# Two swapped neighbours in a hand-written order of steps: a block product against the first product of the next gate, and a vector add against a gate step

## The chip, the cores and the metric

The kernel runs on one core of one Trainium2 chip. The metric is the device time of that core in microseconds (us), from launch to end, as the median of several runs. Five engines work on the core side by side, each in its own order: TensorE (PE in the profile, with its weight loads shown apart as PEld), VectorE (DVE), ScalarE (ACT), GpSimd (POOL), and SyncE (SP), which here only issues transfers.

## What is computed

128 graphs of 128 nodes with 256 features go through four graph layers: attention with four heads, a gated graph network, a relational layer, attention with one head. Each layer is followed by a residual sum and a layer norm. The change lies in the second layer, a GRU that runs three rounds with one set of gate weights:

```python
A = (adj != 0).astype(x.dtype)
h = x
for i in range(3):
    m = jnp.einsum('bnd,de->bne', h, weight[i])
    aggr = jnp.einsum('bst,bsd->btd', A, m)
    gi = aggr @ w_ih.T + b_ih            # i_r, i_z, i_n
    gh = h @ w_hh.T + b_hh               # h_r, h_z, h_n
    r = sigmoid(i_r + h_r)               # reset gate
    z = sigmoid(i_z + h_z)               # update gate
    n = tanh(i_n + r * h_n)              # new state
    h = (1.0 - z) * n + z * h
```

## The kernel before

**Groups and steps.** The graphs are cut into 33 groups: one of 2 graphs, 31 of 4, one of 2. Each stage of the work on one group is a Python generator, and every `yield` ends one step of it. `loads` (L160) brings a group in, `head` (L432) is the first layer, `chunk_0` and `chunk_1` (L680, L683, both through `chunk`, L630) are the two halves of the 256 hidden features of the GRU, `reset_and_new` (L624) and `new_and_update` (L627) make its gates, and `tail` (L686) does the last two layers and the store.

**The order is written out by hand.** Strings of letters say which generator takes its next step. `STEPS` (L61) is one period, 356 letters; the loop at L850 plays it 31 times, each time with the groups moved on by one. In `PERIOD` (L60) a letter names a stage and how far its group lies from that of the period. For the change four letters matter, all of the period's own group: `b` is `chunk_0`, `d` is `chunk_1`, `f` is `reset_and_new`, `g` is `new_and_update`. Since a step emits its instructions when it is called, and L857 to L867 tie each engine's instructions together in the order written, the letters fix the order on every engine. There is no scheduler. `START` and `END` hold what comes before the first and after the last period.

**The gates.** `gates` (L578) multiplies the 2 x 2 blocks of a gate's weights with the 2 x 2 blocks of the state in seven block products, the weight blocks in `factors` and the state's blocks and their sums in `layer[source]`. `f` makes the reset gate r (14 steps in each round) and then the input's part of the new state, "ni" (10 steps); `g` makes the hidden part of the new state, "nh" (10 steps), and then the update gate z (14 steps). A gate takes two PSUM banks of two halves each: `first` holds c11 and c12 (tag `sums`), `second` holds c21 and c22 (tag `gate`). There are two banks of each tag, taken in turn. So z gets the very banks that nh had before it, and z's first product may write only once ScalarE has read nh out of them. In r and z each product comes twice, once for the hidden state (`h`) and once for what the neighbours send (`a`); ni has only `a`, nh only `h`. The steps of a gate, as far as they matter here:

```python
for i, source in enumerate(TERMS[name]):
    product(c21, 1, source, start=i == 0)      # first block product
    yield
    product(c22, 5, source)                    # second block product
    yield
nc.scalar.copy(c11, c21)                       # L600
nc.scalar.copy(p5, c22)                        # L602
yield
... 
nc.vector.tensor_add(c12, c21, p5)             # L610
yield
for source in TERMS[name]:
    product(c12, 3, source)
yield
```

All products are `nc.tensor.matmul` at L590. [...] In the names of the profile `T_a` and `T_h` are sums of state blocks, `agT` is what the neighbours sent, `h0T` and `h2T` are the state after no and after two rounds, and `p_ni`, `p_z` are the `p5` of those gates.

**The two halves of the state.** In `chunk` each round goes: tanh of r on ScalarE (L642), nh out of PSUM on ScalarE (L648), `n = (r + 1) * n` on VectorE (L650), add ni (L652, VectorE), tanh (L654, ScalarE), `d = h - n` (L657, GpSimd), tanh of z (L642), and the new state (L662 and L663, VectorE). L676 copies a transposed state out of PSUM on ScalarE.

Of the kernel before, what the change touches and what calls it, by code (L numbers as in the profile page):

```python
# [58 lines left out]
"""  # L59
PERIOD = {"a": ("v", -1), "b": ("u", 0), "c": ("h", 1), "d": ("v", 0), "e": ("t", -2), "f": ("p", 0), "g": ("q", 0), "h": ("l", -1), "i": ("t", -1), "j": ("t", -3), "k": ("l", 2), "l": ("h", 2), "m": ("l", 0), "n": ("l", 1)}  # L60
STEPS = """  # L61
abcbddbedfggffghgdbiffgecfffdfdfjccccgfffggfbcjgbbgedcdidfgffgffeggfgifcbffegigggjfeibbkggdbgiiecccc
eggbdbibdfcdiiicfgggibeiicbdilbbiifciiickiidgddfiddfgddegfffffieggemginifdfcfibcgifcbdldlcclifffdgge
efggbfcgfgegggecfgfbgfcbfgcdbgbdbgiccclddbfbigdbbcccciddgbbffgiccddddcfdgfigfffffcccccdiffgeggffiggd
dibcfegfiigggffbfbggdfgfggbbfigbgffbldbggdiliilelgddlcil
"""
LAST = {"a": ("v", -2), "b": ("u", -1), "c": ("v", -1), "d": ("p", -1), "e": ("q", -1), "f": ("t", -3), "g": ("t", -2), "h": ("t", -4), "i": ("t", -1), "j": ("l", -2), "k": ("l", -1)}
END = """
# [864 lines left out]
```

## Time and profile before

| What | Value |
|---|---|
| median of 3 runs | 2881.12 us (2878.44 to 2882.46) |
| the profiled execution, its own time | 2883.62 us |
| its span, first to last instruction | 2881.8 us |
| its mean granted TensorE clock | 0.994 |
| PE busy | 2769.5 us, 96% of the span |
| PEld busy | 2287.3 us, 79% |
| DVE busy | 2291.2 us, 80% |
| ACT busy | 1735.7 us, 60% |
| POOL busy | 941.0 us, 33% |

How to read it: a busy share is an average over the whole span. Time is lost where TensorE, in its fixed order, stands before an instruction whose input or whose bank is not ready. The profile lists such idle time under the engine that waited, with what ended it. A weight load runs ahead of its matmul, so a wait often shows as longer idle time on PEld than on PE.

One period of the order lasts 86.5 us: the same matmul, z's first product in the first round, starts at 1073.43 us and at 1159.95 us.

### The profile page before, as it was taken

What the parts mean: (1) busy time and instruction counts of PE and PEld (TensorE: products, weight loads), DVE (VectorE), ACT (ScalarE), POOL (GpSimd) and SP (SyncE); (2) the same over time, 40 slices, a digit from 0 to 9 for tenths busy, and PEclk for the clock granted to TensorE, in tenths of its full rate; (3) what the DMA queues carried; (4) which work ended last, traced back from release to release, by engine and by line L of the source; (5) the groups of instructions that cost most, each with busy time, mean ns of one, the idle gap of its engine ahead of it and who ended that gap; (6) DMA issues with size and microseconds to landing.
All of it is one profiled execution on the core that took longest, in us unless ns stands there. A gap on an engine that the chain in (4) does not pass through costs nothing.

```text
span 2881.8 us, 44849 instructions
## 1 busy us (share of the span) xinstructions
PE 2769.5 (96%) x14486; PEld 2287.3 (79%) x14486; DVE 2291.2 (80%) x5334; ACT 1735.7 (60%) x4440; POOL 941.0 (33%) x925
## 2 busy tenths in 40 slices
PE   6899999999999999999999999999999999999986
PEld 4778888888888888888888888888888888888774
DVE  6677887878887878887878887878888877887765
ACT  3556666556666656666656666656666656666544
POOL 0224333323333323333323333323333423333331
PEclk9999999999999999999999999999999999999998
DMA  3344555444545444545344445344445444445321
GB/s 93 76 82 84 97 103 107 84 92 88 99 99 110 81 92 90 102 96 112 83 89 93 98 96 114 86 83 97 95 96 114 89 80 98 94 96 108 70 56 45
DMA packets 1179216, 264.01 MB, mean 92 GB/s; under 512 B 932064, under 2 KB 1178720, under 8 KB 1178976
## 3 DMA queue, kind: packets, MB, share of 16 engines
q1 hardware_dynamic: 1174448, 257.26, 44.5%
q10 hardware_dynamic: 4528, 3.81, 0.5%
q8 instruction: 118, 1.93, 0.3%
q14 instruction: 122, 1.00, 0.1%
HBM read 153.36 MB, written 107.61 MB: 91 GB/s over the span
## 4 chain that ended last, share of the span: by engine, by line
PE 74%; DVE 19%; issue 2%; ACT 2%; POOL 1%; DMA 1%; SPq 0%; DVEq 0%; POOLq 0%; ACTq 0%
PE gate L590 34%; PE ps L115 20%; PE sums L590 16%; DVE d L662 2%; PE ps L118 2%; DVE h3T L663 2%; DVE gate L618 2%; DVE h2T L663 2%; DVE n L652 1%; DVE aT L512 1%; DVE em L475 1%; DVE h0T L334 1%; DVE em L796 1%; POOL T_h L553 1%; DVE sums L610 1%
## 5 line engine op out<-in xcount | busy, mean ns | idle before, releaser
L590 PE MATMUL gate<-T_a,factors 128*128 128x256 f32 (+1 forms) x2376 | 683.1, 376 | 18.1 <-DVE T_a L553 17.3
L590 PE MATMUL gate<-T_h,factors_h 128*128 128x256 f32 (+1 forms) x2376 | 682.0, 377 | 12.3 <-DVE gate L618 8.9
L590 PEld LDWEIGHTS gate<-T_a,factors 128*128 128x128 f32 x2376 | 438.6, 190 | 91.5 <-DVE T_a L553 29.9
L590 PEld LDWEIGHTS gate<-T_h,factors_h 128*128 128x128 f32 x2376 | 428.6, 190 | 96.2 <-DVE gate L618 37.3
L590 PE MATMUL sums<-agT,factors 128*128 128x256 f32 (+1 forms) x1188 | 356.0, 381 | 5.5 <-ACT sums L600 1.4
L654 ACT ACTIVATE n<-n,bih 128x512 f32<-128x512 f32 (+1 forms) x198 | 139.6, 705 | 258.0 <-DVE n L652 258.0
L600 ACT COPY sums<-gate 128x256 f32<-128x256 f32 (+1 forms) x396 | 139.8, 353 | 228.6 <-PE gate L590 223.3
L590 PEld LDWEIGHTS sums<-agT,factors 128*128 128x128 f32 x1188 | 214.9, 190 | 63.5 <-ACT sums L600 16.8
L361 ACT ACTIVATE x<-x,mr_x,rs_x 128x256 f32<-128x256 f32 x384 | 199.2, 589 | 90.9 <-DVE mr_x L356 90.9
L398 ACT ACTIVATE em<-em,nm 128x128 f32<-128x128 f32 x640 | 248.2, 392 | 8.2 <-DVE nm L395 5.3
L657 POOL TENSOR_TENSOR d<-h1T,n 128x512 f32<-128x512 f32 (+1 forms) x66 | 82.1, 1245 | 500.2 <-ACT n L654 500.2
L715 POOL TENSOR_TENSOR x<-x,x 128x512 f32<-128x512 f32 x63 | 78.9, 1273 | 457.9 <-DVE x L712 255.1
L115 PE MATMUL ps<-wh,aT 128*128 128x64 f32 (+1 forms) x1280 | 191.0, 296 | 1.5 <-DVE aT L512 1.0
L657 POOL TENSOR_TENSOR d<-h2T,n 128x512 f32<-128x512 f32 (+1 forms) x66 | 92.7, 1405 | 286.3 <-ACT n L654 286.3
L590 PE MATMUL gate<-agT,factors 128*128 128x256 f32 (+1 forms) x594 | 180.4, 385 | 3.3 <-ACT r L642 2.5
L115 PEld LDWEIGHTS ps<-wh,aT 128*128 128x128 f32 x1280 | 170.7, 192 | 13.5 <-DVE aT L512 1.2
L573 ACT COPY agT<-ps 128x512 f32<-128x512 f32 (+1 forms) x198 | 114.0, 576 | 97.9 <-PE ps L115 97.7
L650 DVE SCALAR_TENSOR_TENSOR n<-r,n 128x512 f32<-128x512 f32 (+1 forms) x198 | 129.8, 669 | 52.4 <-ACT n L648 52.2
L354 POOL TENSOR_TENSOR rs_x<-rs_x,neghalf 128x4 f32<-128x4 f32 (+1 forms) x99 | 98.5, 995 | 217.4 <-DVE rs_x L353 217.3
L745 POOL TENSOR_TENSOR x<-x,b 128x256 f32<-128x256 f32 x128 | 138.3, 1110 | 68.4 <-PE ps L115 68.4
L610 DVE TENSOR_TENSOR sums<-gate,p_r 128x256 f32<-128x256 f32 (+1 forms) x99 | 42.0, 425 | 141.6 <-PE gate L590 141.5
L115 PE MATMUL ps<-w,x0s 128*128 128x264 f32 x512 | 139.2, 396 | 14.9 <-DMA factors_h<-in_L_gnn_w_hh_dram 14.9
(169 smaller groups left out, 6258.1 us busy)
## 6 DMA issues: line engine op xcount, KB each, us to landing
d_em<-em SPq DMA_DIRECT2D x63, 512.0 KB, 3.4
aT<-d_em SPq DMA_DIRECT2D x252, 128.0 KB, 3.9
x0s<-in_x_dram SPq DMA_DIRECT2D x248, 64.0 KB, 2.5
adj<-in_adj_dram SPq DMA_DIRECT2D x62, 256.0 KB, 3.9
x<-in_x_dram SPq DMA_DIRECT2D x31, 512.0 KB, 4.0
d_h0T<-x SPq DMA_DIRECT2D x62, 256.0 KB, 2.8
h0T<-d_h0T SPq DMA_DIRECT2D x124, 128.0 KB, 3.2
d_h<-h3T SPq DMA_DIRECT2D x62, 256.0 KB, 2.3
```

Of the source, the lines that this page charges most:

```text
L115: nc.tensor.matmul(ps, lhsT, rhs, start=start, stop=stop)
L354: nc.gpsimd.tensor_tensor(rs, rs, neghalf[:, :n], ALU.pow)
L361: nc.scalar.activation(y[:, g, :], y[:, g, :], AF.Identity, bias=mr[:, g : g + 1], scale=rs[:, g : g + 1])
L398: nc.scalar.activation(em[:, r, :], em[:, r, :], AF.Exp, bias=nm[:, i : i + 1], accum_out=den[:, i : i + 1])
L573: nc.scalar.copy(t, ps)
L590: nc.tensor.matmul(into, w[:, SEL[name], k - 1], layer[source][k], start=start, stop=True, skip_group_check=True)
L600: nc.scalar.copy(c11, c21)
L650: nc.vector.scalar_tensor_tensor(n, tr, 1.0, n, ALU.add, ALU.mult)
L654: nc.scalar.activation(n, n, AF.Tanh, bias=bih[:, 2 * C + c : 2 * C + c + 1])
L657: nc.gpsimd.tensor_sub(d, hT, n)
L663: nc.vector.scalar_tensor_tensor(hT, d, 0.5, n, ALU.mult, ALU.add)
L745: nc.gpsimd.tensor_add(x2[:, g, :], x2[:, g, :], b2)
```

## The change

Three lines of letters differ, in three places, each an exchange of two neighbouring letters (positions count from 0):

```
position  58: "g f" becomes "f g"
position 246: "d b" becomes "b d"
position 320: "d f" becomes "f d"
```

```diff
 STEPS = """
-abcbddbedfggffghgdbiffgecfffdfdfjccccgfffggfbcjgbbgedcdidfgffgffeggfgifcbffegigggjfeibbkggdbgiiecccc
+abcbddbedfggffghgdbiffgecfffdfdfjccccgfffggfbcjgbbgedcdidffgfgffeggfgifcbffegigggjfeibbkggdbgiiecccc
 eggbdbibdfcdiiicfgggibeiicbdilbbiifciiickiidgddfiddfgddegfffffieggemginifdfcfibcgifcbdldlcclifffdgge
-efggbfcgfgegggecfgfbgfcbfgcdbgbdbgiccclddbfbigdbbcccciddgbbffgiccddddcfdgfigfffffcccccdiffgeggffiggd
-dibcfegfiigggffbfbggdfgfggbbfigbgffbldbggdiliilelgddlcil
+efggbfcgfgegggecfgfbgfcbfgcdbgbdbgiccclddbfbigbdbcccciddgbbffgiccddddcfdgfigfffffcccccdiffgeggffiggd
+dibcfegfiigggffbfbggfdgfggbbfigbgffbldbggdiliilelgddlcil
 """
```

Counting the letters gives the steps. At 58, `f` takes its 16th step, ni's second block product in the first round (`product(c22, 5, "a")`), and `g` its 11th, z's first block product (`product(c21, 1, "h", start=True)`): on TensorE ni's product now stands ahead of z's. At 246, `d` takes its 30th step, L662 and L663 of the second round on VectorE, and `b` its 29th, the copy of L676 on ScalarE: two engines, so the order on each stays what it was. At 320, `d` takes its 41st step, L650 of the third round for the second half, and `f` its 68th, L610 for ni: on VectorE the add now stands ahead of L650. No step that is exchanged issues a transfer. The orders on ScalarE, GpSimd and SyncE are unchanged, and so are `START` and `END`.

## The prediction

> **What bounds the kernel now.** I read the page's busy rows first, then the chain that ended last, then the list of waits, and last the timeline at the two places where the order of an engine changes.
>
> ```profile
> PE 2769.5 (96%) x14486; PEld 2287.3 (79%) x14486; DVE 2291.2 (80%) x5334; ACT 1735.7 (60%) x4440; POOL 941.0 (33%) x925
> ...
> PE 74%; DVE 19%; issue 2%; ACT 2%; POOL 1%; DMA 1%; SPq 0%; DVEq 0%; POOLq 0%; ACTq 0%
> ```
>
> TensorE bounds the kernel. It is busy 96% of the span, and in the middle more than that: 84.66 us of the 86 us from 1000 to 1086. So only what shortens TensorE's own stream, or a wait in it, shortens the period. VectorE holds 19% of the chain, so there are stretches in which it leads. The list of waits names what stops TensorE:
>
> ```profile
> PE gate L590 <- ACT n L648: 5.7, 32, 0.7
> ...
> PEld gate L590 <- ACT n L648: 18.7, 33, 0.9
> PEld sums L590 <- ACT sums L600: 19.3, 40, 0.8
> PEld sums L590 <- DVE sums L610: 31.2, 99, 0.7
> ```
>
> The columns are total us, times, longest. The first two waits occur about once per period (31 periods). They are those of z's first product (its bank is still being read by L648) and, among others, of ni's third product, which follows the copies L600 and L602. The third, 99 times, is three per period and more.
>
> **The first exchange (position 58), as it runs now.** The timeline of one period, TensorE, its weight loads and ScalarE:
>
> ```profile
> 1071.95 0.70 PE L590 MATMUL gate<-T_h,factors_h 128*128 128x256 f32 x2 [0.16 <-DVE gate L618]
> 1072.58 0.70 PE L590 MATMUL gate<-agT,factors 128*128 128x256 f32 x2
> 1072.69 0.69 ACT L648 ACTIVATE n<-gate,bhn 128x512 f32<-128x512 f32 x1 [0.17 <-PE gate L590]
> 1073.43 0.30 PEld L590 LDWEIGHTS gate<-h0T,factors_h 128*128 128x128 f32 x2 [0.56 <-ACT n L648]
> 1073.43 0.70 PE L590 MATMUL gate<-h0T,factors_h 128*128 128x256 f32 x2 [0.16 <-ACT n L648]
> 1073.76 0.41 PEld L590 LDWEIGHTS gate<-T_a,factors 128*128 128x128 f32 x2
> 1073.97 0.59 PE L590 MATMUL gate<-T_a,factors 128*128 128x256 f32 x2
> 1074.40 0.59 PE L590 MATMUL gate<-T_h,factors_h 128*128 128x256 f32 x2
> 1074.66 0.36 ACT L600 COPY sums<-gate 128x256 f32<-128x256 f32 x1 [1.28 <-PE gate L590]
> 1074.86 0.68 DVE L650 SCALAR_TENSOR_TENSOR n<-r,n 128x512 f32<-128x512 f32 x1
> 1075.07 0.30 PEld L590 LDWEIGHTS sums<-agT,factors 128*128 128x128 f32 x2 [0.47 <-ACT sums L600]
> 1075.07 0.70 PE L590 MATMUL sums<-agT,factors 128*128 128x256 f32 x2
> 1076.23 0.43 DVE L610 TENSOR_TENSOR sums<-gate,p_ni 128x256 f32<-128x256 f32 x1 [0.69 <-PE gate L590]
> ```
>
> A product in a full stream takes 0.43 us from start to start (1073.97 to 1074.40). Two holes are seen. Ni's first product (agT, 1072.58) ends at 1073.28, z's first (h0T) at 1073.43 + 0.70 = 1074.13: 0.85 us later instead of 0.43, because it waits for L648 to leave the bank at 1073.38. Behind it stands ni's second product (T_a), whose inputs are long there, and it ends at 1073.97 + 0.59 = 1074.56. ScalarE has been idle 1.28 us for just that one (L600 starts 0.10 us after it), and TensorE then waits for L600: the product at 1075.07 ends at 1075.77, while the one before it ends at 1074.99, so 0.78 instead of 0.43 us.
>
> After the exchange T_a runs in the hole. agT ends at 1073.28 as now, T_a 0.43 us behind it at 1073.71. The weight load of h0T is released at 1073.43 as now, so h0T ends at 1074.13: nothing lost, and T_h at 1074.56 (0.43 earlier than now). L600 starts at 1073.81, since ScalarE is free from 1073.38, and is done at 1074.17. The next product can load its weights at 1074.22 against 1074.20 in a full stream, and so ends at about 1075.02 instead of 1075.77. TensorE has gained 0.42 + 0.35 less 0.02, that is **0.75 us**.
>
> VectorE then sets the limit. L610 for ni waited 0.69 us for TensorE; with TensorE 0.75 us earlier it is ready at 1075.48, but L650 ahead of it ends only at 1075.54 (from 1070.10 on VectorE has no gap). So L610 and the product behind it move by **0.69 us**, and that is what I take per period.
>
> **Does this reach the period's end?** From 1076.23 VectorE runs without a gap until about 1097.7, and TensorE without a wait of its own in that stretch. Both move together, as all of it hangs on L610 and on TensorE's stream. What does not move are transfers begun before 1072 us. The load of `x` for L712 (1076.58) is issued from 1064.6 to 1066.9 us and lands 3.6 us later, some 6 us early; that of `aT` for L816 (1078.64) is issued by 1069.5 us and takes 2.7 us, some 6 us early; `x0s` is issued by 1076.3 us, lands in 2.5 us, and is needed at 1092.5. None is used up by 1 us. SP's and POOL's orders are untouched, and GpSimd waits for others (14.5 us before L715).
>
> **The second exchange (position 320).** The timeline of the same period:
>
> ```profile
> 1049.06 1.29 DVE L650 SCALAR_TENSOR_TENSOR n<-r,n 128x512 f32<-128x512 f32 x2 [1.01 <-ACT n L648]
> 1049.26 0.59 PE L590 MATMUL gate<-T_a,factors 128*128 128x256 f32 x2
> ...
> 1049.91 0.41 PEld L590 LDWEIGHTS sums<-agT,factors 128*128 128x128 f32 x2
> ...
> 1050.27 0.42 DVE L610 TENSOR_TENSOR sums<-gate,p_ni 128x256 f32<-128x256 f32 x1
> 1050.75 0.30 PEld L590 LDWEIGHTS sums<-agT,factors 128*128 128x128 f32 x2 [0.43 <-DVE sums L610]
> 1051.07 0.41 PEld L590 LDWEIGHTS gate<-T_h,factors_h 128*128 128x128 f32 x2
> 1051.48 0.69 DVE L652 TENSOR_TENSOR n<-n,sums 128x512 f32<-128x512 f32 x1 [0.79 <-PE sums L590]
> 1054.51 0.69 DVE L652 TENSOR_TENSOR n<-n,gate 128x512 f32<-128x512 f32 x1 [1.29 <-PE gate L590]
> ```
>
> The two L650 stand ahead of L610. Its input, T_a, ends at 1049.26 + 0.59 = 1049.85, so L610 could start at 1049.90 instead of 1050.27. TensorE's load at 1050.75 would come at 1050.34 in a full stream (1049.91 + 0.43). After the exchange L610 ends at 1050.32, and the following product's load moves from 1051.07 to 1050.77: **0.30 us** gained. The cost: VectorE waits 0.23 us for TensorE (from 1049.67, where the second of the two 0.68 us L650 starts now, to 1049.90), and the second L650 starts at 1050.25, 0.58 us later than now. It ends by 1050.9; the next use of VectorE, L652, waits for TensorE until 1051.2 even so, and the reader of that L650 is the L652 at 1054.51, which waits 1.29 us today. That cover hides it; without it the price is 0.58 us per period. From 1054.51 to 1064.25 the chain runs through VectorE; it hangs on that L652, and so on TensorE, and moves too. Its transfer, `h0T` for L334 at 1057.88, is issued by 1049.3 us and lands 3.2 us later, 5 us early.
>
> **The third exchange (position 246)** changes no engine's order and no queue: 0.
>
> **The sum.** (0.69 + 0.30) x 31 = 30.7 us. Against the profiled execution's own 2883.62 us (its span 2881.8) this gives 2852.9 us; it ran 2.5 us above the median of 2881.12, so the forecast against the median is 2850.4 us.
>
> [...] Of the hole at 1073.43 the trace shows that the weight load waits too: PEld is idle 0.56 us, and the load of a constant block starts only at the release. [...]
>
> **Rivals.** (1) *Part of it is given back* (chance 0.17). VectorE has no gap from 1070.10 to 1075.54, and once the wait for TensorE is gone none until 1097.7. If these back-to-back instructions have less room than their rows say, or if L600 is not freed by T_a, only the 0.42 us of the first hole or one of the exchanges remains: 0.30 to 0.72 us, 9 to 22 us, 2859 to 2872. For it: some 74 us of VectorE work in 90 (1000 to 1090). Against: ScalarE's start 0.10 us after T_a. (2) *No effect* (0.05): a later wait, such as that for T_a at 1064.25 (0.49 us on PE) or L618 at 1071.95, grows by what is gained. It would have to hang on something before both places; the rows show it behind VectorE work that starts from TensorE. About 2881. (3) *Slower* (0.06): L610, now ahead of the second L650, holds VectorE's queue while it waits. If T_a ended late enough, the second L650 would push L652 and then the 10 us VectorE chain from 1054.51 back. Priced at its 0.58 us per period, with nothing gained at the first place: +18 us, 2899. It decides once the second L650 comes over 1.29 us later than now, the slack of that L652; the trace has 0.58. That the change does nothing is excluded for two exchanges (TensorE's and VectorE's orders do change) and certain for the third.
>
> **Numbers.** The full gain has 0.72: 2845 to 2857 (the gain of 0.99 us taken as 0.8 to 1.15, and the spread of the runs). With most of rival 1 the range is 2844 to 2866. A measurement of this kernel can tell about 0.2%, 5.8 us, from no change. Faster 0.89 (the full gain and rival 1), within it 0.05, slower 0.06.
>
> **What would show it.** Right: in the profile after, the wait of PEld for "ACT n L648" and that for "ACT sums L600" nearly vanish (18.7 and 19.3 us now), that for "DVE sums L610" falls by about 0.4 us per period, and the period is 85.5 instead of 86.5 us; L610 for ni in the first round starts right behind L650. Wrong: these waits vanish and the period stays, with a new wait on PE between 1076 and 1137, or L652 at 1054.51 no longer waits for TensorE but for L650.

## The result, and the profile after

The changed kernel takes 2848.72 us (median of 5 runs, 2846.54 to 2849.61), against 2881.12 us before. The ratio is 0.9887, with a 95% interval of 0.9873 to 0.9902. The forecast was 2850.4 us. The profiled execution has a span of 2847.7 us at a granted clock of 0.994, the same clock as before.

The page after, its busy row:

```profile
PE 2744.5 (96%) x14486; PEld 2292.4 (81%) x14486; DVE 2290.5 (80%) x5334; ACT 1734.5 (61%) x4440; POOL 941.2 (33%) x925
```

VectorE, ScalarE and GpSimd do the same work to within 2 us. PE's busy time falls by 25 us, although it has the same 14486 matmuls to do, so part of the waiting was booked as work. A product shows as two matmuls and two weight loads, a pair (x2 in its rows). A pair's row of 0.59 us reaches 0.16 us beyond the step of 0.43 to the next pair, and so into a wait behind it; and a pair behind a wait is shown 0.11 us longer (0.70). An estimate from these rows: three waits less per period make 3 x 0.27 x 31 = 25.1 us.

The list of waits after, TensorE's weight loads (total us, times, longest):

```profile
PEld gate L590 <- DVE T_a L553: 29.5, 32, 1.5
...
PEld sums L590 <- DVE sums L610: 15.7, 54, 0.7
...
PEld sums L590 <- ACT sums L600: 4.6, 9, 0.8
...
PEld gate L590 <- ACT n L648: 1.2, 2, 0.9
```

The three waits named in the prediction are the three that shrink: for L648 from 18.7 to 1.2 us and from 33 times to 2, for L600 from 19.3 to 4.6 and from 40 to 9, for L610 from 31.2 to 15.7 (0.50 us per period, where about 0.4 was named) and from 99 to 54. Together they lose 47.7 us, more than the time gained, because idle time on PEld starts at the end of the load before: 0.56 us where TensorE lost 0.42. No other wait of its weight loads grows by more than 0.2 us. The wait for T_a (29.9 us before) stays.

The timeline after, first place (position 58):

```profile
1060.21 0.30 PEld L590 LDWEIGHTS gate<-agT,factors 128*128 128x128 f32 x2 [0.32 <-ACT r L642]
1060.21 0.70 PE L590 MATMUL gate<-agT,factors 128*128 128x256 f32 x2
1060.33 0.69 ACT L648 ACTIVATE n<-gate,bhn 128x512 f32<-128x512 f32 x1 [0.17 <-PE gate L590]
1060.53 0.41 PEld L590 LDWEIGHTS gate<-T_a,factors 128*128 128x128 f32 x2
1060.75 0.59 PE L590 MATMUL gate<-T_a,factors 128*128 128x256 f32 x2
1061.07 0.30 PEld L590 LDWEIGHTS gate<-h0T,factors_h 128*128 128x128 f32 x2
...
1061.43 0.36 ACT L600 COPY sums<-gate 128x256 f32<-128x256 f32 x1 [0.41 <-PE gate L590]
...
1061.84 0.39 PEld L590 LDWEIGHTS sums<-agT,factors 128*128 128x128 f32 x2
...
1062.50 0.68 DVE L650 SCALAR_TENSOR_TENSOR n<-r,n 128x512 f32<-128x512 f32 x1
...
1063.11 0.43 DVE L610 TENSOR_TENSOR sums<-gate,p_ni 128x256 f32<-128x256 f32 x1
```

Ni's second product, T_a, runs while L648 empties the bank. z's first product, h0T, loads its weights 0.86 us after agT's (1060.21 to 1061.07), exactly as before (1072.57 to 1073.43), so it has lost nothing. L600 starts 0.09 us after T_a ends at 1061.34, and the next product's weights follow in the stream. From agT's weight load to L610 it is now 2.90 us; before it was 3.66 (1072.57 to 1076.23), from this load:

```profile
1072.57 0.30 PEld L590 LDWEIGHTS gate<-agT,factors 128*128 128x128 f32 x2 [0.32 <-ACT r L642]
```

Second place (position 320):

```profile
1036.99 0.69 DVE L650 SCALAR_TENSOR_TENSOR n<-r,n 128x512 f32<-128x512 f32 x1 [1.01 <-ACT n L648]
...
1037.83 0.43 DVE L610 TENSOR_TENSOR sums<-gate,p_ni 128x256 f32<-128x256 f32 x1
...
1038.17 0.68 DVE L650 SCALAR_TENSOR_TENSOR n<-r,n 128x512 f32<-128x512 f32 x1
1038.71 0.41 PEld L590 LDWEIGHTS gate<-T_h,factors_h 128*128 128x128 f32 x2
...
1039.12 0.69 DVE L652 TENSOR_TENSOR n<-n,sums 128x512 f32<-128x512 f32 x1 [0.27 <-PE sums L590]
```

From the first L650 to the load of T_h it is 1.72 us, before 2.01 (1049.06 to 1051.07). VectorE waits 0.27 us before L652 where it waited 0.79.

**The period.** VectorE's transposition L712 runs once per group in both kernels. The median time from one start of it to the next is 86.16 us before and 85.07 after, 1.09 us less. The 86.5 us given above for one period are one of its longer intervals: most of them lie between 86.13 and 86.17 us.

### The profile page after: what moved, and what is told of

It reads as the page before. It is cut to its first block, busy times and chain, and to the rows that moved or that the text cites. A ratio compares the mean times of both kernels' runs of the same rounds, so it can differ in the third digit from the quotient of the medians.

```text
span 2847.7 us, 44849 instructions
## 1 busy us (share of the span) xinstructions
PE 2744.5 (96%) x14486; PEld 2292.4 (81%) x14486; DVE 2290.5 (80%) x5334; ACT 1734.5 (61%) x4440; POOL 941.2 (33%) x925
## 4 chain that ended last, share of the span: by engine, by line
PE 75%; DVE 19%; issue 2%; POOL 1%; ACT 1%; DMA 1%; SPq 0%; DVEq 0%; POOLq 0%; ACTq 0%
PE gate L590 35%; PE ps L115 21%; PE sums L590 16%; DVE d L662 2%; PE ps L118 2%; DVE h3T L663 2%; DVE gate L618 2%; DVE h2T L663 2%; DVE n L652 1%; DVE aT L512 1%; DVE em L475 1%; DVE h0T L334 1%; DVE em L796 1%; POOL T_h L553 1%; DVE sums L610 1%
## 5 line engine op out<-in xcount | busy, mean ns | idle before, releaser
L590 PE MATMUL gate<-T_h,factors_h 128*128 128x256 f32 (+1 forms) x2376 | 682.0, 377 | 12.3 <-DVE gate L618 8.9
L590 PE MATMUL sums<-agT,factors 128*128 128x256 f32 (+1 forms) x1188 | 344.5, 376 | 2.3 <-ACT sums L600 1.4
L654 ACT ACTIVATE n<-n,bih 128x512 f32<-128x512 f32 (+1 forms) x198 | 139.5, 705 | 248.6 <-DVE n L652 248.6
L600 ACT COPY sums<-gate 128x256 f32<-128x256 f32 (+1 forms) x396 | 139.8, 353 | 204.7 <-PE gate L590 199.3
L657 POOL TENSOR_TENSOR d<-h1T,n 128x512 f32<-128x512 f32 (+1 forms) x66 | 82.1, 1245 | 499.9 <-ACT n L654 499.9
L657 POOL TENSOR_TENSOR d<-h2T,n 128x512 f32<-128x512 f32 (+1 forms) x66 | 92.7, 1405 | 276.9 <-ACT n L654 276.9
L115 PEld LDWEIGHTS ps<-wh,aT 128*128 128x128 f32 x1280 | 170.7, 192 | 13.5 <-DVE aT L512 1.2
L650 DVE SCALAR_TENSOR_TENSOR n<-r,n 128x512 f32<-128x512 f32 (+1 forms) x198 | 132.2, 669 | 52.3 <-ACT n L648 52.2
L610 DVE TENSOR_TENSOR sums<-gate,p_r 128x256 f32<-128x256 f32 (+1 forms) x99 | 42.0, 424 | 141.4 <-PE gate L590 141.3
```

The lines of the kernel that those rows point to most:

```text
L115: nc.tensor.matmul(ps, lhsT, rhs, start=start, stop=stop)
L590: nc.tensor.matmul(into, w[:, SEL[name], k - 1], layer[source][k], start=start, stop=True, skip_group_check=True)
L650: nc.vector.scalar_tensor_tensor(n, tr, 1.0, n, ALU.add, ALU.mult)
L654: nc.scalar.activation(n, n, AF.Tanh, bias=bih[:, 2 * C + c : 2 * C + c + 1])
L657: nc.gpsimd.tensor_sub(d, hT, n)
```

## The experiments

The kernel before was measured again beside each set of runs, with 2878.23, 2879.89 and 2879.20 us. A few us between kernels of different sets are therefore not safe by themselves. Where it matters, the median period (from L712 to L712, as above) is given too, read from each kernel's own trace.

**Each exchange alone.** Three kernels, each with one of the three exchanges on top of the kernel before:

```diff
-...edcdidfgffgffegg...      (position 58 alone)
+...edcdidffgfgffegg...
-...ffbfbggdfgfggbbf...      (position 320 alone)
+...ffbfbggfdgfggbbf...
-...lddbfbigdbbcccci...      (position 246 alone)
+...lddbfbigbdbcccci...
```

> Only the first exchange (TensorE: ni's second block product ahead of z's first, first round of the GRU), the other letters as before. Theory (two holes closed, 0.42 + 0.35 us per period, as the profile after shows 2.90 us from the load of ni's first product to its add L610 in place of 3.66): 0.76 x 31 = 23.6 us less than before, 2857.5 us; the add L610 starts 0.6 us after the L650 ahead of it. Rival A (VectorE without a gap gives only part of it back once the other exchange is missing): less than 18 us gained, above 2863. Rival B (only the bank's hole is worth anything, 0.42 us): 13 us, 2868.

> Only the exchange on VectorE in the third round (add L610 for ni ahead of the second half's L650). Theory (one hole of TensorE closed, 0.29 us per period): 9.0 us less than before, 2872 us, and the sum with the first exchange alone gives the whole of the change. Rival (the 10 us stretch on VectorE behind it takes the gain back): 2881 us, no difference, and the gain of the change would be the first exchange's alone, or the two would work only together.

> Only the exchange of a ScalarE copy with a VectorE step (position 246). Theory: the order on every engine stays, so no difference, 2881 us within 0.1%. Rival (which tile is named first changes a buffer's release or a wait): a difference of more than 3 us, of either sign.

| Kernel | Median | Ratio to before, 95% interval | Period |
|---|---|---|---|
| position 58 alone | 2855.89 us | 0.9918 [0.9903, 0.9934] | 85.36 us |
| position 320 alone | 2868.44 us | 0.9968 [0.9957, 0.9979] | 85.83 us |
| position 246 alone | 2878.15 us | 1.0000 [0.9992, 1.0009] | 86.12 us |
| before, beside these | 2878.23 us | | 86.16 us (the trace of before) |

The first is worth 22.3 us, the second 9.8, the third nothing. Together 32.1 us; the whole change brought 32.4 (2881.12 less 2848.72). In the periods it is 0.80 and 0.33 us, together 1.13, against 1.09 for the whole change. The two gains add within the noise, so neither needs the other. Rival A is out: 22.3 us is over its 18 (the interval begins at 19), and 2855.89 us is below its 2863; so is the bank's hole alone (13 us). The rivals of the other two runs are out as well.

**The opposite of the first exchange.**

```diff
-...edcdidfgffgffegg...
+...edcdidfggffffegg...
```

> The opposite of the first exchange, on top of the kernel before: ni's second block product goes behind both of z's first two products instead of behind one. The bank's hole stays as it is, as z's first product still waits for L648. Theory (ScalarE's copies L600 and L602 hang on that second product, and TensorE's next product on L600): L600 starts 0.43 us later, TensorE's next product too, 0.43 x 31 = 13.3 us more, 2894 us, and the wait of the weight load for L600 doubles from 0.47 to 0.90 us. Rival (only the wait for the bank costs time): no difference, 2881 us.

Measured 2891.74 us, ratio 1.0047 [1.0032, 1.0063]: 13.5 us more than the 2878.23 beside it, where 13.3 were expected. The waits of its weight loads:

```profile
PEld sums L590 <- ACT sums L600: 32.6, 40, 0.9
...
PEld gate L590 <- ACT n L648: 18.7, 33, 0.9
```

The wait for the bank is unchanged (18.7 us). The wait for L600 has grown by 13.3 us, from 19.3. So the second hole is real: ni's second product came 0.43 us later and the period grew by as much, while the bank's hole stayed as it was. ScalarE's copies hang on that product, wherever it stands. A reader who saw only the wait for the bank would have booked 13 us for the first exchange and missed the rest.

**The same exchange on VectorE, in the first round.** On top of the changed kernel, the second half's letter at position 56 (L650) goes behind the one at 67 (L610 for ni):

```diff
-...bbgedcdidffgfgffeggfgifc...
+...bbgedcdiffgfgffeggfdgifc...
```

> On top of the changed kernel the exchange that the change makes on VectorE in the third round is made in the first round as well: the add L610 for ni ahead of the second half's L650. There TensorE is ready only when L650 is just over. Theory (L610 is held by TensorE there and not by L650; the exchange only opens 0.6 us of idle time in a stretch of 20 us in which VectorE has no gap): not faster; 0.3 to 0.6 us more per period, 9 to 19 us, 2858 to 2868. Rival A (my prediction's limit, VectorE holds L610 back): L610 comes earlier and the kernel gets faster by up to 2 us. Rival B (the stretch has room behind it): no difference, 2849.

Measured 2854.41 us, ratio to before 0.9911 [0.9894, 0.9927]; 5.7 us above the changed kernel. The two intervals overlap, but the period is clearly longer, 85.34 against 85.07 us. Its timeline, agT's weight load and VectorE:

```profile
1061.26 0.30 PEld L590 LDWEIGHTS gate<-agT,factors 128*128 128x128 f32 x2 [0.32 <-ACT r L642]
...
1062.41 1.22 DVE L395 TENSOR_REDUCE nm<-em 128x8 f32<-128x1024 f32 x1
1064.16 0.43 DVE L610 TENSOR_TENSOR sums<-gate,p_ni 128x256 f32<-128x256 f32 x1 [0.52 <-PE gate L590]
1064.50 0.68 DVE L650 SCALAR_TENSOR_TENSOR n<-r,n 128x512 f32<-128x512 f32 x1
```

L610 does not come earlier: agT's weight load is at 1061.26, and again it is 2.90 us to L610. So TensorE holds L610 there, not L650, and the prediction's limit (rival A) falls. The exchange only opens 0.52 us of idle time. The size was missed: 9 to 19 us were expected, 5.7 came. Per period 0.27 us of the 0.52 come through, just short of the 0.3 expected (31 times that would be 8.4 us; the last group's interval, with no period behind it, is 1.5 us shorter than in the changed kernel). TensorE's list of waits has a new one:

```profile
PEld ps L115 <- DVE aT L816: 8.8, 29, 0.3
```

Where the rest of the 0.52 us is taken up was not traced. The same exchange of the same two instructions gains in one round (9.8 us) and loses in the other (5.7 us); what decides here is which of the two engines is late.

**How far does the cover reach?** On top of the changed kernel, the L650 that the change pushed back goes back further (the letter at position 321 behind the one at 333):

```diff
-...fbfbggfdgfggbbfigbgffbldbg...
+...fbfbggfgfggbbfigbgfdfbldbg...
```

> On top of the changed kernel the L650 of the third round's second half, which the change pushed back by about 0.5 us, is pushed back another 2.6 us, behind L652, L610 for z and L618 for ni, into the 1.3 us in which VectorE waits for TensorE. Theory (this L650 is wholly covered up to that L652 which reads it): no difference to the changed kernel, 2848.7 us within 3 us, and the wait before the L652 shrinks from 1.3 to about 0.6 us. Rival (the step pushed back is what the change pays with): 0.1 to 0.6 us more per period, 2852 to 2867.

This theory fell: 2858.60 us, ratio to before 0.9925 [0.9908, 0.9941], 9.9 us above the changed kernel; the period is 85.50 us against 85.07. The number is the rival's, but the reason is another. Its timeline:

```profile
1130.23 0.43 DVE L618 TENSOR_TENSOR gate<-gate,p_ni 128x256 f32<-128x256 f32 x1
...
1130.46 1.26 POOL L657 TENSOR_TENSOR d<-h2T,n 128x512 f32<-128x512 f32 x1 [6.44 <-ACT n L654]
1130.58 1.70 DVE L650 SCALAR_TENSOR_TENSOR n<-r,n 128x512 f32<-128x512 f32 x1
...
1132.38 0.69 DVE L652 TENSOR_TENSOR n<-n,gate 128x512 f32<-128x512 f32 x1
```

L650 takes 1.70 us instead of 0.68, and L652 behind it no longer waits for TensorE: L650 is the late one. It starts 0.12 us after GpSimd's L657 and ends 0.56 us after that has ended (1131.72 to 1132.28), as if it had stood still meanwhile. This is so in every period: its 186 full-size rows of L650 take 159.1 us, those of the changed kernel 127.3, which is 31 times 1.03 us more. The delay reaches TensorE over ScalarE: the tanh L654 behind that L652 comes later, with it the copy L423 behind L654, and TensorE waits for L423 (12.3 us in all, against 1.5 in the changed kernel):

```profile
PE ps L115 <- ACT rows L423: 12.3, 33, 1.2
```

Two more runs test this by leaving out that subtraction alone:

```diff
-            nc.gpsimd.tensor_sub(d, hT, n)
+            if l == L - 1 and c == 0:
+                nc.gpsimd.memset(d, 0.0)
+            else:
+                nc.gpsimd.tensor_sub(d, hT, n)
```

> The kernel with L650 pushed back by 2.6 us, in which that L650 took 1.70 us instead of 0.68 beside GpSimd's subtraction L657, with this subtraction left out in the third round's first half: GpSimd fills the tile with zeros instead and reads nothing (h - n is missing there, all else stays). Theory (L650, with two inputs in SBUF, stood still until GpSimd's L657 was done): L650 takes 0.68 us again, VectorE waits some 0.6 us for TensorE before the L652, and the time is that of the changed kernel with the same part left out, within 3 us; some 10 us less than with the subtraction. Rival (the place of L650 costs by itself): 2858 us as with the subtraction.

> The changed kernel with the same subtraction left out (GpSimd fills the tile with zeros in the third round's first half). It is there to be compared with: nothing else runs beside that subtraction that it could hold up, and its result comes 1.2 us before it is read, so both theories expect the time of the changed kernel, 2848.7 us within 3 us.

With L650 pushed back, 2848.29 us (0.9889 [0.9873, 0.9906]); with L650 where the change has it, 2847.41 us (0.9887 [0.9871, 0.9904]). The two agree, also in their periods (85.07 and 85.08 us), and the first is 10.3 us below the run with the subtraction. Its VectorE timeline:

```profile
1039.01 0.68 DVE L650 SCALAR_TENSOR_TENSOR n<-r,n 128x512 f32<-128x512 f32 x1
1040.39 0.69 DVE L652 TENSOR_TENSOR n<-n,gate 128x512 f32<-128x512 f32 x1 [0.70 <-PE gate L590]
```

L650 is back at 0.68 us and VectorE waits 0.70 us again. So it was not the place of L650 by itself that cost 9.9 us but that place together with the GpSimd instruction beside it.

**One more wait.** The list of waits after still has T_a, once per period. On top of the changed kernel, the letter at position 2 (the step of L413 to L416) goes behind the one at 18 (the first L553 of T_a):

```diff
-abcbddbedfggffghgdbiff...
+abbddbedfggffghgdbciff...
```

> On top of the changed kernel one more step is moved on VectorE, at the start of the period: the four small operations L413 to L416 (1.7 us together) go behind the first L553 of the neighbours' sums, T_a, for which TensorE waits once per period (0.49 us on PE, 0.89 us of weight load). Their own reader, the transpose at L420, comes some 1.1 us later on TensorE. Theory (a wait of TensorE is closed by putting what it waits for ahead of work that nobody waits for yet): up to 0.87 us per period, some 25 us less than the changed kernel, 2824 us (2820 to 2833). Rival (the transpose at L420 takes over as the wait, or VectorE's long stretch leads anyway): less than 9 us, above 2840.

Measured 2824.04 us, ratio to before 0.9810 [0.9794, 0.9826]: 24.7 us below the changed kernel, and the fastest version here (period 84.30 us against 85.07). The wait in the changed kernel:

```profile
1051.89 0.30 PEld L590 LDWEIGHTS gate<-T_a,factors 128*128 128x128 f32 x2 [0.89 <-DVE T_a L553]
```

The timeline of VectorE and TensorE with the letter moved:

```profile
1037.22 0.41 DVE L553 TENSOR_TENSOR T_a<-ps,agT 128x256 f32<-128x256 f32 x1
1037.56 0.36 DVE L413 CAST split<-wh 128x16 bf16<-128x16 f32 x1
...
1038.54 0.41 PEld L590 LDWEIGHTS gate<-T_a,factors 128*128 128x128 f32 x2
...
1038.76 0.59 PE L590 MATMUL gate<-T_a,factors 128*128 128x256 f32 x2
...
1039.71 0.10 PEld L420 LDWEIGHTS <-split 128*48 128x48 bf16 x1 [0.33 <-DVE T_a L553]
```

T_a is ready 0.91 us before its product loads weights, and the product runs in the stream (loads at 1038.12, 1038.54, 1038.97). The transpose at L420 has the same 0.33 us of idle time before it as in the kernel before.

## Why the prediction was right

**The first hole and the second.** Forecast: T_a fills the hole of 0.42 us, and L600 is freed early, 0.35 us more. The timeline after shows both. The first exchange alone brought 22.3 us, or 0.72 per period, which the first hole alone (13 us) does not reach; and moving T_a the other way lengthened the second hole alone, by 0.43 us. How the gain divides between the two holes is read from the timeline; no run fills one of them alone.

**VectorE's limit of 0.69 us** is the one term of this sum that was mis-sized. L610 moved by 0.76 us (3.66 to 2.90). I let L610 start at the end of the row of L650; in the trace it starts 0.61 us after L650's start, 0.07 before that row ends. With that overlap the two limits fall together to 0.01 us. The run in the first round shows that TensorE alone holds L610 to the same 2.90 us, so its 0.75 us was the figure to take.

**The second exchange**, 0.30 us per period: the timeline shows 0.29 (2.01 to 1.72 us), the run alone 9.8 / 31 = 0.32. The push back of L650 (forecast 0.58 us) cost nothing: VectorE still waits 0.27 us for TensorE before the next L652.

**The third exchange**, 0: measured 0.

**The sum.** 0.76 + 0.29 = 1.05 us per period, times 31 is 32.6 us; measured 32.4, forecast 30.7. From one weight load of z's first product to the next it is 85.44 us (1061.07 to 1146.51), where 85.5 was forecast and 86.52 measured before.

```profile
1146.51 0.30 PEld L590 LDWEIGHTS gate<-h0T,factors_h 128*128 128x128 f32 x2
```

That the gain reaches the period's end was argued from VectorE's unbroken stretch and from the early transfers; the period, shorter by 1.09 us at the median, shows it.

**The weight loads behind a wait.** In the trace of before the loads that waited for L648, L600 and L610 start only when the wait ends, each together with its matmul (at 1073.43, 1075.07 and 1050.75), and the pair behind the first of them follows after 0.54 us (1073.43 to 1073.97) instead of 0.43. The forecast counts these 0.11 us in each of the three waits removed. Without them it would be 0.99 - 3 x 0.11 = 0.66 us per period, 20.5 us, an estimate from the same rows. The 32.4 us measured (28 to 37 by the interval) agree with the count that has them.

**The rivals.** Partial loss, no effect and slower did not come. Rival 3's threshold does not hold in general, though. I put it at 1.29 us, the whole of VectorE's idle time before the L652. That idle time was no room for this instruction: GpSimd's L657 runs into that very time, and an L650 of 0.68 us, put there, took 1.70. How far L650 can be delayed in the place that the change gives it was not tried. In the changed kernel L650 ends at 1038.85, 1.8 us before L657 starts (1040.64), so the change does not meet this; the prediction had not looked at it.

## What to carry to other kernels

In an order written by hand, look at each wait of the bounding engine and ask two things: which ready instruction stands right behind the waiting one (let it pass), and which instruction that nobody waits for yet stands ahead of the releaser on its own engine (let the releaser pass). Book both ends of such a move: the instruction that fills a hole may itself release another engine earlier, which here, by the timeline, was almost half of the first exchange's gain (0.35 of 0.76 us). Before moving work into another engine's idle time, look at what the neighbours run in that time, and before copying an exchange to a similar place, look which side is late there.

## What the runs showed of the hardware

VectorE's L650 (two inputs in SBUF, 128x512) took 0.68 us alone and 1.70 us when it started 0.12 us after GpSimd's L657 of 1.26 us, and 0.68 us again when nothing ran on GpSimd in that time. The timeline of the changed kernel has the counterpart, GpSimd and VectorE at the same time:

```profile
1125.70 1.27 POOL L657 TENSOR_TENSOR d<-h2T,n 128x512 f32<-128x512 f32 x1 [6.44 <-ACT n L654]
...
1125.81 0.42 DVE L618 TENSOR_TENSOR gate<-gate,p_ni 128x256 f32<-128x256 f32 x1
```

L618 takes only one of its inputs from SBUF, the other from PSUM. It starts 0.11 us after L657, too, and takes its usual 0.42 us. So beside L657 the L650 took 1.02 us longer and the L618 no longer than usual. L650's end lies 0.56 us behind L657's, as it would if all but 0.12 us of its own 0.68 came after L657 was done. Why the one was held up and the other not is not shown: the two differ in size (128x512 and 128x256) and in operation as well as in where their inputs lie. Nor does any run here separate L657's reading from the rest of what it does.
